# A four-layer graph network on one core: another order between graphs, adjacency in four pieces, elu without GpSimd

## The chip, the core and the metric

One core of a Trainium2 chip runs the whole program. The time is device microseconds of one execution, as a median of several; the profile page belongs to one further execution. TensorE (PE) does the matrix products, VectorE (DVE) and ScalarE (ACT) the element-wise work, GpSimd (POOL) small things, and SyncE (SP) issues transfers.

## What is computed

32 independent graphs of 512 nodes with 256 features each pass four layers. Each layer normalizes the features, takes relu, runs a graph attention, and adds its result to the features. All arithmetic is in float32.

```python
def reference(x, adj, ...):                 # x: 32 x 512 x 256, adj: 32 x 512 x 512 int32
    # layer 0: score = (h W_att) h^T / 16, softmax under the mask, two tanh convolutions
    h = relu(layernorm(x));  x = x + L0(h, adj)
    # layer 1: e = leaky(src_i + dst_j), masked softmax, attention @ Wh
    h = relu(layernorm(x));  x = x + L1(h, adj)
    # layer 2: e = exp(-leaky(s_i + d_j)) where adj != 0, rows divided by their sum, then elu
    h = relu(layernorm(x));  x = x + elu((e @ Hh) / rowsum)
    # layer 3: logits = Ax_j + Ay_i + h a_12 h^T, leaky, masked softmax, two products, then elu
    h = relu(layernorm(x));  x = x + elu(h W_1 + (attention @ h) W_2)
```

elu(y) is y for y > 0 and exp(y) - 1 otherwise. It can be written max(y, 0) + min(exp(y), 1) - 1.

## The kernel before

The kernel describes every graph as a list of small operations, each with an engine, a cost that the author took as typical, and the operations it comes after. A plan then fixes, ahead of the run, in which order each engine gets them. Up to four graphs are in flight, and the features of a fifth may be loaded. On the chip each engine runs its list strictly in order and waits where an input isn't there. The plan decides only the order; the chip decides the times.

```python
class Plan:
    PASS = 200.0
    SLACK = {"V": (1.05, 0.0), "A": (1.05, 0.0), "G": (1.5, 0.0), "D": (1.0, 800.0)}
    ...
    def order(self, pools):
        ...
        for o in reversed(self.ops):
            o["way"] += o["cost"][1] + self.PASS          # way: cost to the end of its graph
            o["rank"] = (o["graph"], -o["way"], o["number"])
            for a in o["after"]:
                if a["graph"] == o["graph"]:
                    a["way"] = max(a["way"], o["way"])
        ...                                               # each engine takes its ready operation of lowest rank
```

Loads are issued from GpSimd (only those of graph 0 from SyncE). SyncE issues the transposing transfers: of the class codes of the adjacency (codeT), of the normalized features in two 16-bit planes (planesT), and of a row of maxima (crest).

```python
def fetch(what):
    T[what] = loaded.pop((what, b)) if b == 0 else load(what, b, nc.gpsimd)

got_x = op("G", G_LOAD_X, [ends[b - FLIGHT - 1]] if b > FLIGHT else [], partial(fetch, "x"))
got_adj = op("G", G_LOAD_ADJ, [code_before], partial(fetch, "adj"))        # 1 MB in one transfer
```

Layer norm, before each layer's products: statistics and variance on DVE, the power -0.5 on GpSimd, offset on DVE, relu and scale on ACT, split in planes on DVE, transposing transfer, and the join into hT on ACT.

```python
def root(g):
    nc.gpsimd.tensor_tensor(T[f"rstd{l}"][:, two(g)], T[f"ve{l}"][:, two(g)], mhalf[:, two(g)], ALU.pow)   # L379
def norm(t):
    nc.scalar.activation(T[f"xn{l}"][:, t, :], T["x"][:, t, :], AF.Relu, bias=..., scale=...)              # L386
def split(t, place):
    nc.vector.tensor_copy(p, bits)                                                                         # L392
def turn(t, place):
    nc.sync.dma_start_transpose(out=p, in_=...)                                                            # L397
def join(t):
    nc.scalar.copy(bits[...], ...)                                                                         # L401
```

The products by name: fp features (layers 0 and 3), vp values with score columns, qk and gk the score matrices, row the scores transposed onto all partitions, av attention times values, zp and op the second convolution of layer 0, hw the own features of layer 3. In layers 1 and 2 the scores become eT through two ACT operations (L478, L482) and one masking operation on DVE (L614, L649).

The elu of layer 2 and of layer 3:

```python
# layer 2, per tile t of 128 nodes
def lower():   nc.vector.tensor_scalar(y2[t], av2[t], rs2[t], 0.0, ALU.mult, ALU.min)               # L661
def upper():   nc.scalar.activation(r2[t], av2[t], AF.Relu, scale=rs2[t])                           # L665
# per pair g of tiles
def exp2(g):   nc.scalar.activation(y2[g], y2[g], AF.Exp)                                           # L671
def add_r(g):  nc.gpsimd.tensor_add(x[g], x[g], r2[g])                                              # L674
def add_e(t):  nc.vector.scalar_tensor_tensor(x[t], y2[t], -1.0, x[t], ALU.add, ALU.add)            # L678
# layer 3, per pair
def lower3(g): nc.vector.tensor_scalar(r3[g], y3[g], 0.0, None, ALU.min)                            # L783
def upper3(g): nc.vector.scalar_tensor_tensor(x[g], y3[g], 0.0, x[g], ALU.max, ALU.add)             # L786
def exp4(g):   nc.scalar.activation(r3[g], r3[g], AF.Exp)                                           # L790
def both(g):   nc.vector.scalar_tensor_tensor(y3[g], r3[g], -1.0, x[g], ALU.add, ALU.add)           # L793
```

Of the kernel before, what the change touches and what calls it, by code (L numbers as in the profile page):

```python
# [11 lines left out]
F32 = mybir.dt.float32  # L12
I32 = mybir.dt.int32
# [6 lines left out]
P = 128  # L20
# [14 lines left out]
    return t, t + 170.0  # L35


V_STATS, V_XN, V_TINY, V_TWO, V_SCALE5 = (525.0, 610.0), (322.0, 407.0), (80.0, 165.0), (255.0, 340.0), (402.0, 486.0)
V_MASK, V_CODE, V_HALF, V_PSUM, V_ADD = (602.0, 683.0), (600.0, 690.0), (600.0, 690.0), (395.0, 484.0), (334.0, 425.0)
A_COPY, A_HALF, A_PRELU, A_EXP, A_TANH = (477.0, 597.0), (253.0, 373.0), (570.0, 693.0), (519.0, 640.0), (373.0, 474.0)  # L40
A_BIAS, A_PRELU2 = (570.0, 687.0), (629.0, 722.0)
G_POW, G_ADD, G_STORE = (981.0, 1017.0), (1230.0, 1267.0), (900.0, 900.0)
A_NORM, A_JOIN, V_SPLIT = (491.0, 590.0), (620.0, 767.0), (332.0, 422.0)
D_TURN = (1310.0, 2600.0)
G_LOAD_X, G_LOAD_ADJ = (1000.0, 6000.0), (1000.0, 9000.0)


class Plan:
# [2 lines left out]

    PASS = 200.0

    SLACK = {"V": (1.05, 0.0), "A": (1.05, 0.0), "G": (1.5, 0.0), "D": (1.0, 800.0)}

    def __init__(self):
# [22 lines left out]
    def order(self, pools):  # L81
        free = {pool: list(range(n)) for pool, n in pools.items()}
        users = {}
        for o in self.ops:
            o["left"] = len(o["after"])
            for a in o["after"]:
                users.setdefault(a["number"], []).append(o)
        for o in reversed(self.ops):
            o["way"] += o["cost"][1] + self.PASS
            o["rank"] = (o["graph"], -o["way"], o["number"])  # L90
            for a in o["after"]:
                if a["graph"] == o["graph"]:
                    a["way"] = max(a["way"], o["way"])
        engines = sorted({o["engine"] for o in self.ops})
        ready = {e: [] for e in engines}
        at = dict.fromkeys(engines, 0.0)
        events = []
        numbers = itertools.count()
        for o in self.ops:
            if not o["left"]:  # L100
                heapq.heappush(ready[o["engine"]], (o["rank"], o))
        now, out = 0.0, []
        while True:
            for e in engines:
                skipped = []
                while at[e] <= now and ready[e]:
                    rank, o = heapq.heappop(ready[e])
                    need = [p["pool"] for p in o["takes"]]
                    if any(len(free[n]) < need.count(n) for n in need):
                        skipped.append((rank, o))  # L110
                        continue
                    for p in o["takes"]:
                        p["number"] = free[p["pool"]].pop(0)
                    holds, until = o["cost"]
                    at[e] = now + holds
                    out.append(o)
                    heapq.heappush(events, (at[e], next(numbers), None))
                    heapq.heappush(events, (now + until + self.PASS, next(numbers), o))
                for x in skipped:
                    heapq.heappush(ready[e], x)  # L120
            if not events:
                break
            now = events[0][0]
            while events and events[0][0] <= now:
                o = heapq.heappop(events)[2]
                if o is None:
                    continue
                for r in o["reads"]:
                    r["readers"] -= 1
                    if not r["readers"]:  # L130
                        free[r["pool"]].append(r["number"])
                for w in users.get(o["number"], []):
                    w["left"] -= 1
                    if not w["left"]:
                        heapq.heappush(ready[w["engine"]], (w["rank"], w))
        assert len(out) == len(self.ops), "the plan is stuck"
        return out, now
# [3 lines left out]
def kernel(  # L141
# [41 lines left out]
    ps = ctx.enter_context(tc.tile_pool(name="ps", bufs=1, space=PSUM))  # L183


    def load(what, b, queue):
        if what == "x":
            t = io.tile([P, NT, H], F32, tag="x", name=f"x_{b}")
            queue.dma_start(out=t, in_=x[b].rearrange("(t p) h -> p t h", p=P))
        else:  # L190
            t = io.tile([P, NT, N], I32, tag="adj", name=f"adj_{b}", bufs=1)
            queue.dma_start(out=t, in_=adj[b].rearrange("(t p) m -> p t m", p=P))
        return t

    loaded = {("x", 0): load("x", 0, nc.sync), ("adj", 0): load("adj", 0, nc.sync)}


    ident = const.tile([P, P], F32, tag="ident", name="ident")
# [67 lines left out]

    zero = const.tile([P, 1], F32, tag="zero", name="zero")
    nc.gpsimd.memset(zero, 0.0)
    transposed(l1_sb, l1_aug[:, :, :H])
    for o in range(2):  # L270
        product(lambda d: l1_aug[:, d, H + o : H + o + 1], l1_sb,
# [43 lines left out]
    def graph(b, before, code_before):  # L315
# [25 lines left out]
            return slice(2 * g, 2 * g + 2)  # L341


        def fetch(what):
            T[what] = loaded.pop((what, b)) if b == 0 else load(what, b, nc.gpsimd)

        got_x = op("G", G_LOAD_X, [ends[b - FLIGHT - 1]] if b > FLIGHT else [], partial(fetch, "x"))
        got_adj = op("G", G_LOAD_ADJ, [code_before], partial(fetch, "adj"))

        def classes(g):  # L350
            nc.vector.tensor_scalar(T["code"][:, two(g), :], T["adj"][:, two(g), :], -1.0, 2.0, ALU.max, ALU.min)
# [3 lines left out]

        turned, code, rows_code = [], None, plan.place("code")
        for g in range(NT // 2):
            code = op("V", V_CODE, begin + [got_adj, code], partial(classes, g), takes=[] if code else [rows_code])
            turned += [op("D", D_TURN, [code], partial(turn_code, t), reads=[rows_code]) for t in (2 * g, 2 * g + 1)]

        def mask0():
# [291 lines left out]
        def third(t, a, place):  # L653
            def sums():
                rs = T["rs2"][:, t : t + 1]

                nc.vector.tensor_scalar(rs, T[f"av2{t}"][:, H : H + 1], LEAST, None, ALU.max)
                nc.vector.reciprocal(rs, rs)

            def lower():  # L660
                nc.vector.tensor_scalar(T["y2"][:, t, :], T[f"av2{t}"][:, :H], T["rs2"][:, t : t + 1], 0.0,  # L661
                                        ALU.mult, ALU.min)

            def upper():
                nc.scalar.activation(T["r2"][:, t, :], T[f"av2{t}"][:, :H], AF.Relu, scale=T["rs2"][:, t : t + 1])  # L665

            a = op("V", V_TWO, [a], sums)
            return (op("V", V_PSUM, [a], lower, reads=[place]), op("A", A_TANH, [a], upper, reads=[place]))

        def exp2(g):  # L670
            nc.scalar.activation(T["y2"][:, two(g), :], T["y2"][:, two(g), :], AF.Exp)  # L671

        def add_r(g):
            nc.gpsimd.tensor_add(T["x"][:, two(g), :], T["x"][:, two(g), :], T["r2"][:, two(g), :])  # L674

        def add_e(t):
            xt = T["x"][:, t, :]
            nc.vector.scalar_tensor_tensor(xt, T["y2"][:, t, :], -1.0, xt, ALU.add, ALU.add)  # L678

        free, us = attend(2, es, vs, third)  # L680
        xs = []
        for g in range(NT // 2):
            a = op("A", A_EXP, [l for l, _ in us[two(g)]], partial(exp2, g))
            r = op("G", G_ADD, [u for _, u in us[two(g)]], partial(add_r, g))
            xs += [op("V", V_ADD, [a, r], partial(add_e, 2 * g + j)) for j in range(2)]

# [64 lines left out]
        for g in range(NT // 2):  # L753
# [8 lines left out]
                                         l3_w1s[:, c, :], start=(c == 0), stop=(c == HC - 1))  # L762

            def own_out(g):
                nc.scalar.copy(T["w3"][:, two(g), :].rearrange("p t h -> p (t h)"), T[f"hw{g}"])

            a = op("PE", pe(n256=8), [*hs[two(g)], hi[0]], partial(own, g, place), takes=[place])
            hv.append(op("A", A_COPY, [a], partial(own_out, g), reads=[place]))


        def fourth(t, a, place):
# [7 lines left out]
            a = op("V", V_TINY, [a], sums)  # L779
            return op("V", V_PSUM, [a, hv[t // 2]], both_terms, reads=[place])  # L780

        def lower3(g):
            nc.vector.tensor_scalar(T["r3"][:, two(g), :], T["y3"][:, two(g), :], 0.0, None, ALU.min)  # L783

        def upper3(g):
            nc.vector.scalar_tensor_tensor(T["x"][:, two(g), :], T["y3"][:, two(g), :], 0.0, T["x"][:, two(g), :],  # L786
                                           ALU.max, ALU.add)

        def exp4(g):
            nc.scalar.activation(T["r3"][:, two(g), :], T["r3"][:, two(g), :], AF.Exp)  # L790

        def both(g):
            nc.vector.scalar_tensor_tensor(T["y3"][:, two(g), :], T["r3"][:, two(g), :], -1.0,  # L793
                                           T["x"][:, two(g), :], ALU.add, ALU.add)

        _, us = attend(3, es, vs, fourth)
        last = []
        for g in range(NT // 2):
            l = op("V", V_SCALE5, us[two(g)], partial(lower3, g))
            u = op("V", V_MASK, us[two(g)], partial(upper3, g))  # L800
            l = op("A", A_EXP, [l], partial(exp4, g))
            last.append(op("V", V_MASK, [l, u], partial(both, g)))

        def store():
# [45 lines left out]
```

The softmax here doesn't subtract the row's maximum and nothing guards it: scores larger than these inputs give would overflow.

## Time and profile before

| | |
|---|---|
| time, median of 3 | 2651.21 us (2650.39 to 2652.82) |
| span of the profiled execution | 2653.5 us |
| TensorE clock granted, mean | 0.983 |
| HBM read, written | 52.96 MB, 16.78 MB |
| adjacency loads from GpSimd | 31 of 1024 KB, 6.4 us median to landing |
| feature loads from GpSimd | 31 of 512 KB, 5.0 us |
| turns of planes from SyncE | 512, 2.5 us |

A group on the page reads: line, engine, operation, output <- input, shape, count, then busy time and mean ns of one, then the idle time of the engine just before it and what ended most of it. In the page's row of slices each digit is the busy share of one fortieth of the span in tenths. A line of waits reads: who waited, for whom, microseconds in total, how many times, the longest. In the table of windows each engine has its busy time and its number of instructions, and after the engines come the granted TensorE clock, the busy share of the transfer engines and GB/s.

### The profile page before, as it was taken

The numbers are of one execution on the slowest core, as the hardware profiler recorded it, in microseconds if no ns is written. First come the engines' busy times: TensorE is split into PE (matmuls) and PEld (weight loads), VectorE is DVE, ScalarE is ACT, GpSimd is POOL, SyncE is SP. The second block draws the span as 40 slices with busy tenths as digits, with TensorE's granted clock in tenths as the row PEclk, the third lists the DMA queues.
The fourth block names the chain that finished last, engine by engine and source line by source line (L and its number), as shares of the span: only waits on it lengthen the run. The fifth ranks groups of instructions, "written<-read, shape, count | busy, mean of one in ns | idle before, by whom it ended". The sixth has DMA issues, their size and how long they took to land. (4 is left out here: it accounts for less than half of the span.)

```text
span 2653.5 us, 30679 instructions
## 1 busy us (share of the span) xinstructions
PE 2531.3 (95%) x9548; PEld 1793.5 (68%) x9548; DVE 1713.0 (65%) x5174; ACT 1612.9 (61%) x3041; POOL 367.5 (14%) x426
## 2 busy tenths in 40 slices
PE   5999999999999999999999999999999999999986
PEld 4677767767667666766666776766776667666664
DVE  4467766666676666766567765666766667656664
ACT  2466766676666566665566656666666656656563
POOL 1011111011111011111111110111111111101110
PEclk8999999999999999999999999999999999999998
DMA  5323322123332223332233313233222332222111
GB/s 160 71 37 71 76 70 66 39 58 76 70 70 52 46 67 70 74 64 45 51 72 72 72 37 60 68 72 71 59 51 52 74 66 69 50 58 41 36 36 28
DMA packets 406035, 164.07 MB, mean 62 GB/s; under 512 B 386288, under 2 KB 389360, under 8 KB 405872
## 3 DMA queue, kind: packets, MB, share of 16 engines
q1 hardware_dynamic: 384032, 93.94, 19.4%
q0 software_dynamic: 17504, 65.54, 8.1%
q10 hardware_dynamic: 4336, 2.63, 0.4%
q8 instruction: 76, 1.25, 0.2%
q14 instruction: 87, 0.71, 0.1%
HBM read 52.96 MB, written 16.78 MB: 26 GB/s over the span
## 5 line engine op out<-in xcount | busy, mean ns | idle before, releaser
L501 PE MATMUL av<-v,eT 128*128 128x257 f32 x4096 | 1000.4, 385 | 39.3 <-DVE eT L614 24.2
L501 PEld LDWEIGHTS av<-v,eT 128*128 128x128 f32 x4096 | 779.3, 192 | 239.7 <-issue 97.3
L401 ACT COPY hT<-planesT 128x512 uint16<-128x512 uint16 x512 | 377.5, 765 | 131.1 <-DMA planesT<-planes 130.5
L379 POOL TENSOR_TENSOR rstd<-ve,mhalf 128x2 f32<-128x2 f32 x256 | 213.7, 851 | 1662.3 <-DVE ve L376 1417.7
L453 PE MATMUL vp<-l_aug,hT 128*128 128x258 f32 (+1 forms) x1536 | 397.7, 389 | 39.5 <-ACT hT L401 39.5
L453 PEld LDWEIGHTS vp<-l_aug,hT 128*128 128x128 f32 x1536 | 294.0, 194 | 123.4 <-ACT hT L401 53.5
L386 ACT ACTIVATE xn<-x,off,rstd 128x256 f32<-128x256 f32 x512 | 281.8, 595 | 92.8 <-DVE off L382 92.4
L392 DVE COPY planes<-xn 128x512 uint16<-128x512 uint16 x512 | 213.5, 428 | 101.4 <-ACT xn L386 79.2
L460 ACT COPY v<-vp 128x256 f32<-128x256 f32 x384 | 141.4, 373 | 177.1 <-PE vp L453 138.2
L568 PE MATMUL zp<-eT,y 128*128 128x512 f32 x512 | 241.3, 594 | 3.4 <-ACT y L557 3.3
L457 DVE COPY sd<-vp 128x2 f32<-128x2 f32 (+1 forms) x384 | 56.8, 155 | 289.9 <-ACT v L460 163.3
L538 PE MATMUL qk<-fa,hT 128*128 128x512 f32 x512 | 239.1, 592 | 0.0
L700 PE MATMUL gk<-hT,fa 128*128 128x512 f32 x512 | 224.9, 592 | 0.0
L372 DVE BATCH_NORM_STATS2 st<-x 128x6 f32<-128x256 f32 x512 | 209.1, 408 | 8.2 <-DMA x<-in_x_dram 8.2
L478 ACT ACTIVATE eT<-row,sd 128x512 f32<-128x512 f32 x256 | 164.4, 688 | 42.5 <-PE row L474 42.5
L700 PEld LDWEIGHTS gk<-hT,fa 128*128 128x128 f32 x512 | 97.2, 190 | 111.9 <-issue 106.9
L704 DVE SCALAR_TENSOR_TENSOR eT<-gk,sd,mask 128x512 f32<-128x512 f32 x128 | 96.0, 750 | 116.1 <-PE gk L700 116.0
L482 ACT ACTIVATE eT<-eT 128x512 f32<-128x512 f32 x256 | 151.8, 636 | 0.0
L542 ACT ACTIVATE eT<-qk 128x512 f32<-128x512 f32 x128 | 75.2, 598 | 123.9 <-PE qk L538 123.9
L568 PEld LDWEIGHTS zp<-eT,y 128*128 128x128 f32 x512 | 94.8, 191 | 80.1 <-issue 67.0
L736 ACT ACTIVATE eT<-eT,zero 128x512 f32<-128x512 f32 x128 | 85.3, 715 | 99.1 <-DVE crest L714 99.1
L538 PEld LDWEIGHTS qk<-fa,hT 128*128 128x128 f32 x512 | 93.7, 190 | 75.7 <-issue 67.5
(88 smaller groups left out, 3114.6 us busy)
## 6 DMA issues: line engine op xcount, KB each, us to landing
adj<-in_adj_dram POOLq DMA_DIRECT2D x31, 1024.0 KB, 6.4
out_dram<-y POOLq DMA_DIRECT2D x32, 512.0 KB, 3.4
x<-in_x_dram POOLq DMA_DIRECT2D x31, 512.0 KB, 5.0
planesT<-planes SPq DMA_TRANSPOSE x512, 2.5
codeT<-code SPq DMA_TRANSPOSE x128, 3.2
adj<-in_adj_dram SPq DMA_DIRECT2D x1, 1024.0 KB, 11.7
crest<-crest SPq DMA_TRANSPOSE x64, 2.4
x<-in_x_dram SPq DMA_DIRECT2D x1, 512.0 KB, 4.7
```

What stands on the lines that cost most here:

```text
L372: nc.vector.bn_stats(T[f"st{l}"][:, t, :], T["x"][:, t, :])
L379: nc.gpsimd.tensor_tensor(T[f"rstd{l}"][:, two(g)], T[f"ve{l}"][:, two(g)], mhalf[:, two(g)], ALU.pow)
L386: nc.scalar.activation(T[f"xn{l}"][:, t, :], T["x"][:, t, :], AF.Relu, bias=T[f"off{l}"][:, t : t + 1], scale=T[f"rstd{l}"][:, t : t + 1])
L392: nc.vector.tensor_copy(p, bits)
L401: nc.scalar.copy(bits[:, :, :, t * P : (t + 1) * P], T[f"planesT{l}{t}"].rearrange("p (b c) n -> p b c n", b=2))
L453: nc.tensor.matmul(p[:, :cols], T[f"hT{l}"][:, c, t * P : (t + 1) * P], w_aug[:, c, :], start=(c == 0), stop=(c == HC - 1))
L478: nc.scalar.activation(T[f"eT{l}"][:, c, :], T[f"row{l}"], AF.Prelu, bias=T[f"sd{l}"][:, 1, c : c + 1], alpha=ALPHA)
L482: nc.scalar.activation(e, e, AF.Exp, scale=sign)
L501: nc.tensor.matmul(p[:, : H + 1], T[f"eT{l}"][:, c, t * P : (t + 1) * P], v[:, c, :], start=(c == 0), stop=(c == NT - 1))
L538: nc.tensor.matmul(p, T["hT0"][:, k, c * P : (c + 1) * P], T["fa0"][:, k, :], start=(k == 0), stop=(k == HC - 1))
L568: nc.tensor.matmul(p, T["y0"][:, c, k * P : (k + 1) * P], T["eT0"][:, c, :], start=(c == 0), stop=(c == NT - 1))
L700: nc.tensor.matmul(p, T["fa3"][:, k, c * P : (c + 1) * P], T["hT3"][:, k, :], start=(k == 0), stop=(k == HC - 1))
```

## The change

Four things are changed.

1. **Order.** The rank of an operation is no longer (graph, way left) but one number: graph times 40 us, minus the way left. Operations of neighbouring graphs are equal in rank when the younger one has 40 us more to go. For the last graphs the distance is 10 us. The aim is that the graphs in flight keep a fixed distance, so that they are in different layers at any time.
2. **Loads.** All loads are issued by SyncE, and a graph's adjacency comes in four pieces of 256 KB; the class codes of a pair of tiles need only their two pieces. Loads of graph 0 are operations of the plan like the others.
3. **Elu of layer 2.** ACT takes exp and relu straight from the product, DVE adds min(exp, 1) and relu - 1 to the features. GpSimd adds nothing any more, and nothing is done by pairs.
4. **Elu of layer 3.** The -1 is put into w3 by a bias when ACT copies it out, so y3 holds y - 1; exp gets a bias of 1, and the separate minimum is gone.

The assumed cost of the power on GpSimd is lowered too (981/1017 to 800/850 ns), which touches the order alone.

```diff
+    APART, APART_LAST = 40000.0, 10000.0
...
+        last = max(o["graph"] for o in self.ops)
         for o in reversed(self.ops):
             o["way"] += o["cost"][1] + self.PASS
-            o["rank"] = (o["graph"], -o["way"], o["number"])
+            late = max(0, o["graph"] - last + 2)
+            o["rank"] = ((o["graph"] - late) * self.APART + late * self.APART_LAST - o["way"], o["number"])
...
-        got_x = op("G", G_LOAD_X, [ends[b - FLIGHT - 1]] if b > FLIGHT else [], partial(fetch, "x"))
-        got_adj = op("G", G_LOAD_ADJ, [code_before], partial(fetch, "adj"))
+        got_x = op("D", D_X, [ends[b - FLIGHT - 1]] if b > FLIGHT else [], fetch_x)
+        got_adj = [code_before]
+        for t in range(NT):
+            got_adj.append(op("D", D_ADJ if b else D_ADJ0, got_adj[-1:], partial(fetch_adj, t)))
...
-            code = op("V", V_CODE, begin + [got_adj, code], partial(classes, g), takes=[] if code else [rows_code])
+            code = op("V", V_CODE, begin + [got_adj[2 * g + 2], code], partial(classes, g), takes=[] if code else [rows_code])
...
             def lower():
-                nc.vector.tensor_scalar(T["y2"][:, t, :], T[f"av2{t}"][:, :H], T["rs2"][:, t : t + 1], 0.0,
-                                        ALU.mult, ALU.min)
+                nc.scalar.activation(T["y2"][:, t, :], T[f"av2{t}"][:, :H], AF.Exp, scale=T["rs2"][:, t : t + 1])
...
+            def add_lower():
+                xt = T["x"][:, t, :]
+                nc.vector.scalar_tensor_tensor(xt, T["y2"][:, t, :], 1.0, xt, ALU.min, ALU.add)
+
+            def add_upper():
+                xt = T["x"][:, t, :]
+                nc.vector.scalar_tensor_tensor(xt, T["r2"][:, t, :], -1.0, xt, ALU.add, ALU.add)
...
-        def exp2(g):
-            nc.scalar.activation(T["y2"][:, two(g), :], T["y2"][:, two(g), :], AF.Exp)
-
-        def add_r(g):
-            nc.gpsimd.tensor_add(T["x"][:, two(g), :], T["x"][:, two(g), :], T["r2"][:, two(g), :])
...
             def own_out(g):
-                nc.scalar.copy(T["w3"][:, two(g), :].rearrange("p t h -> p (t h)"), T[f"hw{g}"])
+                nc.scalar.activation(T["w3"][:, two(g), :].rearrange("p t h -> p (t h)"), T[f"hw{g}"], AF.Identity,
+                                     bias=minus)
...
-        def lower3(g):
-            nc.vector.tensor_scalar(T["r3"][:, two(g), :], T["y3"][:, two(g), :], 0.0, None, ALU.min)
...
         def exp4(g):
-            nc.scalar.activation(T["r3"][:, two(g), :], T["r3"][:, two(g), :], AF.Exp)
+            nc.scalar.activation(T["r3"][:, two(g), :], T["y3"][:, two(g), :], AF.Exp, bias=one)
```

## The prediction

> **What bounds the kernel now.** I read the page's engine totals and its row of 40 slices first, then a table of windows, then the waits of TensorE alone, then the timeline. The totals and the TensorE row:
>
> ```profile
> PE 2531.3 (95%) x9548; PEld 1793.5 (68%) x9548; DVE 1713.0 (65%) x5174; ACT 1612.9 (61%) x3041; POOL 367.5 (14%) x426
> ...
> PE   5999999999999999999999999999999999999986
> ```
>
> TensorE is busy 95%, nothing else above 68%. But "busy" at which pace? The timeline, in a stretch without gaps, gives the pitch (start, duration, line, group; the next start minus this one, over the count):
>
> ```profile
> 68.28 1.03 PE L501 MATMUL av<-v,eT 128*128 128x257 f32 x4
> 69.14 1.89 PE L523 MATMUL vp<-w_sb,hT 128*128 128x256 f32 x8
> 70.87 1.03 PE L501 MATMUL av<-v,eT 128*128 128x257 f32 x4
> ```
>
> 0.86/4 = 0.217 us for 257 columns (unrounded), 1.73/8 = 0.216 for 256. The same reading elsewhere gives 0.430 for 512 columns and 0.110 for the 128-column transposes. With the counts of the groups: 5632 of 257 or 258 columns x 0.217 = 1222; 1536 of 256 x 0.216 = 332; 2048 of 512 x 0.430 = 881; 256 transposes x 0.110 = 28; the 76 of the prologue 10. Sum **2472.6 us**, which the change doesn't touch: it neither adds nor removes a matmul. So 2653.5 - 2472.6 = **180.9 us** is what can be won at all, and the question is where it lies.
>
> The trace has all 9548 matmuls, and TensorE runs them in program order, so I laid them on a scale of pitch time and read off how far that scale moved in each stretch. Lost (stretch minus progress): 0 to 100 us 39.4; 100 to 500 -0.3, so there TensorE runs at exactly its pitch; 500 to 2500 93.4; 2500 to the end 48.4. The windows (PE, PEld, DVE, ACT, POOL busy; clock; DMA) show the same shape:
>
> ```profile
> 200.00:300.00 100.00, 100.00 (x408) 75.30 (x407) 72.71 (x212) 68.98 (x132) 13.71 (x15) 1.00 0.26 55
> ...
> 1000.00:1100.00 100.00, 95.60 (x361) 68.50 (x360) 68.07 (x206) 61.02 (x117) 15.19 (x18) 0.97 0.32 66
> ...
> 2000.00:2100.00 100.00, 94.62 (x352) 66.21 (x352) 61.85 (x189) 63.38 (x122) 12.59 (x14) 0.98 0.30 60
> ...
> 2500.00:2600.00 100.00, 87.58 (x336) 62.73 (x334) 64.76 (x193) 59.87 (x113) 11.99 (x13) 0.97 0.15 30
> 2600.00:2654.00 54.00, 31.66 (x88) 20.42 (x88) 19.46 (x46) 16.16 (x28) 2.29 (x3) 0.75 0.13 34
> ```
>
> Neither DVE nor ACT is fuller where TensorE stalls than at 200 us where it doesn't. These are latency gaps, not another engine's bound. TensorE's waits name them:
>
> ```profile
> PE vp L453 <- ACT hT L401: 39.5, 22, 6.2
> PE av L501 <- DVE eT L614: 24.2, 15, 3.9
> PE wpp L263 <- DMA l_ac<-in_L_gnn_a_dram: 18.2, 1, 18.2
> PE av L501 <- ACT eT L742: 7.3, 2, 6.9
> ```
>
> By form, 38.4 of the 39.5 are the 257-column kind: layer 3's first product, waiting for the layer norm behind layer 2. L614 is the mask of layer 1. And the tail:
>
> ```profile
> 2604.41 2.08 PE L453 MATMUL vp<-l_aug,hT 128*128 128x257 f32 x4 [6.15 <-ACT hT L401]
> 2607.61 2.08 PE L453 MATMUL vp<-l_aug,hT 128*128 128x257 f32 x4 [1.13 <-ACT hT L401]
> ...
> 2616.71 1.03 PE L453 MATMUL vp<-l_aug,hT 128*128 128x257 f32 x4
> ...
> 2634.99 10.25 PE L501 MATMUL av<-v,eT 128*128 128x257 f32 x32 [6.92 <-ACT eT L742]
> ```
>
> The last graph runs alone; after a gap the same four matmuls take 2.08 us instead of 1.03.
>
> **What the skill says.** "TensorE: Matmul & The Clock Gate", HAM oscillation: a gap longer than about 3.4 us drops the clock to half until TensorE has been busy again. The trace agrees (2.08 against 1.03), so a gap costs more than its length: in 500 to 2500 the waits add up to about 61 us, the loss is 93. "Perfetto Trace Analysis", Optimization Strategy: where the contended engine changes between regimes, interleave them. Layers 0 and 3 here are TensorE's, layers 1 and 2 ACT's (below). "GPSIMD Engine Reference", Engine selection: elementwise adds belong on VectorE. The trace agrees: 1272 ns for the add at L674, 684 ns for a 128x512 add on DVE at L786. "DMA: Bandwidth & Descriptors", Issuing engines are not separate DMA queues: moving a load to another issuer gives no bandwidth. No run before tests that.
>
> **Part 1, the order.** Rank was (graph, -way): the oldest graph always first. Now it is graph x 40 us - way, so a younger graph overtakes an older one that has less left to do. I compared both programs' TensorE order on the pitch scale. Before, every graph looks different. After, graphs 4 to 26 repeat one pattern of 76.9 us, with four graphs at four different layers. Distance on TensorE from the last producer to the first consumer, before (graphs 10 to 25) and after (steady):
> - av of layer 2 to vp of layer 3: 7 to 14 us, **36.7 after**
> - transposed scores to av, layer 1: 2.6 to 5.2, then 5.2
> - av of layer 1 to vp of layer 2: -6 to 12 (pairs overlap), then 17.3
> - op to vp of layer 1: 16 to 20, then 15.0
> - gk to av of layer 3: 15 to 17, then 21.9
> - fp to qk: 2.6 to 21, then 1.9; zp to op: 1.8 to 19, then 2.7
>
> The chain behind the first is, from the groups' means: sums 0.31, relu 0.47, GpSimd add 1.27, DVE add 0.42, statistics 0.59, variance 0.18, root 0.85, offset 0.19, norm 0.60, planes 0.43, turn 2.5, join 0.77: 8.6 us, plus queueing. It doesn't fit 7 us and fits 36.7 four times. Layer 1's chain (0.69 + 0.64 + 0.72 = 2.05 us, plus queueing) was tight at 2.6 and isn't at 5.2. The two that shrink are one copy each (0.59 us); before, zp to op at 1.8 cost 0.6 us in all, fp to qk nothing. So both large waits vanish, and with them the clock drops. I leave 8 us of the 93.4: **-85**.
>
> **Part 2, the end.** The last graphs get a distance of 10 us, so 29, 30 and 31 go abreast: their last av end at 2454, 2465 and 2473 on the pitch scale, against 2396, 2448 and 2473. Behind TensorE's end stay about 8 us (now 2645.2 to 2653.5). But layers 1 and 2 now bunch: between its copies of vp13 and vp20 of graph 31, ACT has 58 instructions, about 0.47 us each back to back = 27 us, beside 26 us of TensorE work; never fully packed, I give 10 us. Two edges are short (0.1 and 0.9 us for a chain of 2.05): 4. Low clock after these: 4. 8 + 10 + 4 + 4 = 26 instead of 48.4: **-22**.
>
> **Part 3, the loads.** Four x loads of 0.5 MB leave GpSimd's queue for SyncE's, and adjacency comes in pieces. The first 20 us move 292 GB/s over three queues, and TensorE waits 18.2 us for a vector on ACT's queue. With two queues ACT's share should rise; I guess 4 us. Then at 39.2 us GpSimd issued 1 MB of adjacency into graph 0's turns (6.8 us to land, median 2.5) and fp waited 3.5 us; now those turns go before graph 1's first piece: 3.5 us. Against this about 4 us for new tight places between 100 and 130 (row to av of layer 2 in graph 0 at 1.7 us). 39.4 becomes 36: **-3.5**. In the steady state SyncE gets 160 loads of about 0.5 us issue, 80 us in all, on a queue that isn't bound.
>
> **Part 4, the elu.** Off GpSimd go 64 adds (81.4 us) and 62 load issues (49.3). DVE: L661's 56.2 and L783's 26.8 go, 128 adds of 0.415 = 53.1 come: -30. ACT: L671's 40.4 goes, 128 exps of 0.473 = 60.5 come; biases lengthen w (0.58 to about 0.68) and r: +30. The chain becomes 7.7 us. With 36.7 us of room that is worth nothing in the middle, and ACT at 1643 us stays under 65%: **0**, or a us at the tail, inside part 2.
>
> **Sum.** 2472.6 + 36 + 8 + 26 = **2543 us**.
>
> **Rivals.** (a) The gaps move: some edge of the fixed pattern is short on the chip, say a turn stuck behind an adjacency piece on SyncE's queue. The pattern repeats some 25 times, so 2 us a graph cost 50: about 2593. For it: SyncE now mixes loads and turns in one queue. Against: 100 to 500 us shows no loss with distances no larger. (b) ACT becomes the bound in the middle, +30 us of work and an in-order engine: about 2580. Against: 51 us of ACT in a period of 77. (c) The start gets worse: SyncE waits for landings between loads and holds graph 0's turns: +10, 2553. (d) Everything hides and the end packs too: 2520.
>
> **Range and chances.** The 2472.6 and about 8 us at the end are sure, the start's 30 nearly. What is open mostly adds. I take 2520 to 2585; two per cent faster is 2598, which needs rival (a) to miss.
>
> **What would show it.** Right: windows from 200 to 2300 with PE at 99 to 100 and clock 1.00; the waits on L453 and L614 below 10 us in sum; the last vp of layer 3 without a 6 us gap; about 77 us from one store to the next. Part 3 right: the first matmul before 18 us. Wrong: a wait that shows up 25 to 28 times, or ACT over 70% there.

## The result, and the profile after

| | before | after |
|---|---|---|
| median | 2651.50 us | **2539.45 us** |
| range | 2650.39 to 2652.82 (4 runs) | 2536.70 to 2540.03 (4 runs) |
| ratio | | **0.9575**, 95% interval 0.9559 to 0.9592 |
| profiled execution | 2653.5 us | 2534.9 us, granted clock 0.994 |

112 us came off; 108 were predicted. The page of the changed kernel, engine totals and the row of slices:

```profile
PE 2489.7 (98%) x9548; PEld 1784.5 (70%) x9548; DVE 1676.7 (66%) x5110; ACT 1630.0 (64%) x3105; POOL 259.1 (10%) x302
...
PE   7999999999999999999999999999999999999998
```

TensorE went from 95 to 98% busy, and only the first slice is below 8 tenths. VectorE lost 36 us of work and ScalarE gained 17; over the shorter span their shares went from 65 to 66% and from 61 to 64%.

The windows (PE, PEld, DVE, ACT, POOL busy; clock; DMA share; GB/s) answer those shown of before:

```profile
1000.00:1100.00 100.00, 100.00 (x376) 70.08 (x375) 64.86 (x196) 63.61 (x120) 9.59 (x11) 1.00 0.27 66
...
2000.00:2100.00 100.00, 100.00 (x376) 69.97 (x375) 64.67 (x196) 63.76 (x121) 9.58 (x11) 1.00 0.31 66
...
2400.00:2500.00 100.00, 94.19 (x357) 67.87 (x356) 69.16 (x216) 76.51 (x150) 7.71 (x10) 0.97 0.17 37
2500.00:2535.00 35.00, 26.71 (x118) 22.02 (x116) 19.81 (x43) 11.60 (x18) 2.31 (x3) 0.94 0.17 53
```

At 1000 and at 2000 us TensorE has no gap and the full clock, with the other engines about as full as before. From 2400 to 2500 ScalarE rises to 76.5: the last graphs' layers 1 and 2 bunch towards the end. In the three stretches of 10 us around TensorE's longest waits there, ScalarE is full or nearly, and at 2320 VectorE too:

```profile
2320.00:2330.00 10.00, 5.30 (x15) 4.08 (x16) 9.60 (x33) 10.00 (x20) 3.43 (x4) 0.66 0.51 119
2400.00:2410.00 10.00, 6.47 (x26) 5.11 (x25) 6.67 (x17) 9.28 (x18) 0.80 (x1) 0.83 0.13 28
2440.00:2450.00 10.00, 7.80 (x30) 6.13 (x29) 6.40 (x25) 9.97 (x21) 1.06 (x1) 0.83 0.32 53
```

TensorE's waits (in total, times, longest):

```profile
PE wpp L267 <- DMA l_ac<-in_L_gnn_a_dram: 13.3, 1, 13.3
PE av L517 <- DVE eT L630: 8.5, 3, 4.2
PE vp L539 <- ACT hT L417: 5.3, 1, 5.3
```

The two large waits of before, on the line of vp (39.5 us, 38.4 of them layer 3's) and on layer 1's mask (24.2 us), became 2.1 (none of it layer 3's) and 8.5 us; the 8.5 lie at the start (1.1) and at the end (7.4).

I use the pitch scale of the prediction again: the time of a stretch minus the pitch time of the matmuls done in it is what TensorE lost there. In us, for the two kernels and the experiments up to e5, which are described below:

| kernel | 0-100 | 100-250 | 250-2350 | 2350-end | sum | median time |
|---|---|---|---|---|---|---|
| before | 39.4 | -0.1 | 90.5 | 51.1 | 181 | 2651.5 |
| after | 27.3 | 9.2 | 7.0 | 19.0 | 62.5 | 2539.5 |
| order alone (e1) | 37.8 | -0.1 | 10.7 | 21.0 | 69 | 2545.1 |
| loads and elu, old order (e2) | 29.9 | 17.7 | 11.0 | 46.8 | 105 | 2579.6 |
| order and elu, old loads (e3) | 37.0 | -0.1 | 8.3 | 18.6 | 64 | 2539.1 |
| order and loads, old elu (e4) | 29.1 | 10.4 | 6.9 | 18.2 | 65 | 2538.8 |
| before without adjacency loads (f1) | 33.1 | 0.3 | 37.7 | 50.6 | 122 | 2597.9 |
| loads alone (f2) | 29.7 | 18.8 | 25.2 | 58.4 | 132 | 2606.1 |
| elu alone (f3) | 38.5 | 0.6 | 45.1 | 55.6 | 140 | 2615.4 |
| 40 us at the end (e5) | 30.8 | 9.5 | -1.5 | 44.3 | 83 | 2557.6 |

Where the new order has its 7 to 11 us in the column 250-2350, they lie after 2300 us and belong to the end (after: -1.2 from 250 to 2300, 27.2 from there on); only e1 loses some 4 us before 2300.

### The profile page after: what moved, and what is told of

Read it like the earlier page. It is cut to its first block, busy times and chain, and to the rows that moved or that the text cites. A ratio compares the mean times of both kernels' runs of the same rounds, so it can differ in the third digit from the quotient of the medians.

```text
span 2534.9 us, 30658 instructions
## 1 busy us (share of the span) xinstructions
PE 2489.7 (98%) x9548; PEld 1784.5 (70%) x9548; DVE 1676.7 (66%) x5110; ACT 1630.0 (64%) x3105; POOL 259.1 (10%) x302
## 4 chain that ended last, share of the span: by engine, by line
PE 94%; issue 3%; DVE 2%; ACT 1%; DMA 0%; POOL 0%; POOLq 0%; ACTq 0%
PE av L517 33%; PE vp L469 13%; PE zp L584 9%; PE qk L554 9%; PE fp L444 8%; PE gk L712 8%; PE vp L539 4%; PE op L603 4%; PE hw L773 4%; PE row L490 1%; PE wpp L267 1%; DVE st L388 0%; DMA l_ac<-in_L_gnn_a_dram 0%; DMA w_sb<-in_L_gnn_W_dram 0%; ACT eT L494 0%
## 5 line engine op out<-in xcount | busy, mean ns | idle before, releaser
L517 PE MATMUL av<-v,eT 128*128 128x257 f32 x4096 | 960.6, 381 | 15.3 <-DVE eT L630 8.5
L395 POOL TENSOR_TENSOR rstd<-ve,mhalf 128x2 f32<-128x2 f32 x256 | 232.7, 910 | 2055.7 <-DVE ve L392 1984.7
L417 ACT COPY hT<-planesT 128x512 uint16<-128x512 uint16 x512 | 384.5, 773 | 72.3 <-DMA planesT<-planes 70.7
L469 PE MATMUL vp<-l_aug,hT 128*128 128x258 f32 (+1 forms) x1536 | 378.1, 381 | 2.1 <-ACT hT L417 2.1
L402 ACT ACTIVATE xn<-x,off,rstd 128x256 f32<-128x256 f32 x512 | 290.9, 608 | 44.3 <-DVE off L398 43.8
L554 PE MATMUL qk<-fa,hT 128*128 128x512 f32 x512 | 233.9, 592 | 0.0
L539 PE MATMUL vp<-w_sb,hT 128*128 128x256 f32 x512 | 122.9, 383 | 5.3 <-ACT hT L417 5.3
L539 PEld LDWEIGHTS vp<-w_sb,hT 128*128 128x128 f32 x512 | 96.1, 192 | 39.3 <-issue 23.1
```

The lines of the kernel that those rows point to most:

```text
L417: nc.scalar.copy(bits[:, :, :, t * P : (t + 1) * P], T[f"planesT{l}{t}"].rearrange("p (b c) n -> p b c n", b=2))
L469: nc.tensor.matmul(p[:, :cols], T[f"hT{l}"][:, c, t * P : (t + 1) * P], w_aug[:, c, :], start=(c == 0), stop=(c == HC - 1))
L517: nc.tensor.matmul(p[:, : H + 1], T[f"eT{l}"][:, c, t * P : (t + 1) * P], v[:, c, :], start=(c == 0), stop=(c == NT - 1))
L539: nc.tensor.matmul(p[:, j * H : (j + 1) * H], T["hT0"][:, c, t * P : (t + 1) * P], w0_sb[:, c, :], start=(c == 0), stop=(c == HC - 1))
L554: nc.tensor.matmul(p, T["hT0"][:, k, c * P : (c + 1) * P], T["fa0"][:, k, :], start=(k == 0), stop=(k == HC - 1))
```

## The experiments

Each ran four times beside the kernel before on the same chip. Before's median was 2652.3 with e1 to e4, 2653.6 with f1 to e5, 2653.0 with e6, e7 and g2, 2649.6 with e9.

### Each part put in or taken out (e1 to e4)

Theory: the order makes the time; loads and elu are worth a few us. Rival: the loads or the elu do part of it by shortening the chain itself.

**e1, the order alone**: before, with the new rank.

```diff
-            o["rank"] = (o["graph"], -o["way"], o["number"])
+            late = max(0, o["graph"] - last + 2)
+            o["rank"] = ((o["graph"] - late) * self.APART + late * self.APART_LAST - o["way"], o["number"])
```

> The kernel before with the new rank alone (loads and elu as before). Theory D, the distance on TensorE between producer and consumer is what counts: the loss of 93 us in the middle goes wholly, the start stays at 39 us and has some tight places behind it (about 10 us: in this order the distance from op to vp of layer 1 is 1.0 us in graph 3), the end loses about 27: 2472 + 39 + 10 + 0 + 27 = 2548 us (2538 to 2560). Rival U, the shorter elu and the loads carry the gain: about 2620 us or more.

Measured: 2545.05 us (2543.57 to 2546.46), ratio 0.9596 (0.9582 to 0.961). The order alone brings 107 of the 112 us.

**e2, everything but the order**: after, with the old rank (the same diff backwards).

> The changed kernel with the old rank (oldest graph first): loads from SyncE in pieces and the new elu alone. Theory D: the start gains some 10 us, the chain is 0.9 us shorter, but the distances from av of layer 2 to vp of layer 3 are again 5 to 12 us and uneven, so the middle loses about 90 us and the end about 48: 2472 + 30 + 90 + 48 = 2640 us (2620 to 2660). Rival U: near 2560 us.

Measured: **2579.59 us** (2577.63 to 2582.42), ratio 0.9727 (0.9711 to 0.9744). This expectation missed by 60 us. With the old order, loads and elu together (and the lowered assumed cost of the power, which e2 keeps) bring 73 us, and TensorE's middle loses 11 us instead of 90. So my reason was incomplete: the middle can be freed by the order, and also without it.

**e3, the old loads in the changed kernel** (1 MB of adjacency and x on GpSimd's queue):

```diff
-            got_adj.append(op("D", D_ADJ if b else D_ADJ0, got_adj[-1:], partial(fetch_adj, t)))
+        got_adj = op("G", G_LOAD_ADJ, [code_before], partial(fetch, "adj"))
```

> The changed kernel with the loads of before (GpSimd, adjacency in one piece of 1 MB). Theory: only the start knows the loads. TensorE's first matmul goes back from 13.3 to about 18 us and graph 0's first products to about 41 to 48 us; start loss 39 instead of 27, the middle loses nothing, the end 27: 2545 us (2538 to 2555). Rival: the 1 MB pieces disturb the turns in the middle too, some us per graph: 2580 us or more.

Measured: 2539.11 us (2538.07 to 2541.16), ratio 0.9575 (0.956 to 0.9589), the same as after. The table says why: the start to 100 us is 10 us worse, 37.0 instead of 27.3, and the filling from 100 to 250 is 9 us better, nothing instead of 9.2.

**e4, the old elu in the changed kernel** (the removed lines of the diff put back):

```diff
-                nc.vector.scalar_tensor_tensor(xt, T["r2"][:, t, :], -1.0, xt, ALU.add, ALU.add)
+            nc.gpsimd.tensor_add(T["x"][:, two(g), :], T["x"][:, two(g), :], T["r2"][:, two(g), :])
```

> The changed kernel with both elus of before (GpSimd additions, minimum before exp). Theory: with 16 us and more of TensorE work between av of layer 2 and vp of layer 3 the longer chain is hidden; the same time as the changed kernel within 8 us: 2540 us (2534 to 2550). Rival: GpSimd's additions of 1.27 us hold up its roots, or the shorter chain was needed: 2560 us or more.

Measured: 2538.76 us (2538.06 to 2540.28), ratio 0.9573 (0.9559 to 0.9587): the elu is worth nothing on top of the rest. e3 and e4 are both 6 us faster than e1. Each of them has one of the two small parts, and both have the lowered assumed cost of the power, which e1 has not; so which of the three brings the 6 us is not shown. By the table they lie after 250 us: e1 loses 31.7 us from there on, e3 26.9 and e4 25.1.

### What filled the chain under the old order (f1 to f3)

e2 asked for a new theory. In before's trace I looked at one of the long waits. GpSimd issues a 1 MB load of adjacency:

```profile
1021.45 0.97 POOL L192 DMA_DIRECT2D adj<-in_adj_dram  x1
```

Just then SyncE issues the turns of layer 3's norm:

```profile
1022.84 1.26 SPq L397 DMA_TRANSPOSE planesT<-planes  x1
1024.14 1.87 SPq L354 DMA_TRANSPOSE codeT<-code  x1
1026.11 4.49 SPq L397 DMA_TRANSPOSE planesT<-planes  x3
```

ScalarE waits for them, and TensorE for ScalarE:

```profile
1030.02 0.76 ACT L401 COPY hT<-planesT 128x512 uint16<-128x512 uint16 x1 [3.93 <-DMA planesT<-planes]
```
```profile
1030.83 2.08 PE L453 MATMUL vp<-l_aug,hT 128*128 128x257 f32 x4 [3.54 <-ACT hT L401]
```

The turn of 1022.84 lands 7.2 us later, just before its use at 1030.02; the median is 2.5. Theory C: the 1 MB loads collide with the turns. Rival E: the chain is long by itself, through the GpSimd addition and the queues.

**f1, before without the adjacency loads.** The order on every engine stays before's. All graphs use graph 0's adjacency, so 31 loads of 1 MB are left out, and with them GpSimd's time to issue them (0.97 us in the line above); the output is another.

```diff
-            T[what] = loaded.pop((what, b)) if b == 0 else load(what, b, nc.gpsimd)
+            if what == "adj":
+                T[what] = loaded[("adj", 0)]
+            else:
+                T[what] = loaded.pop((what, b)) if b == 0 else load(what, b, nc.gpsimd)
```

> The kernel before with its order, its elu and its GpSimd queue as they were; only the 31 adjacency loads of 1 MB for graphs 1 to 31 are left out (every graph uses graph 0's adjacency, so the output is not the reference's). Theory C (the middle was lost because the 1 MB load collides with the turns of layer 3's norm, which then land late, once or twice a graph): most of the 93 us in the middle goes, 2570 to 2600, with layer 3's vp waiting below 15 us in sum. Rival E (the chain behind layer 2 is long by itself, through the GpSimd addition and the queues on the engines, and loads have little to do with it): 2630 to 2650, vp still waiting 30 us or more.

Measured: 2597.9 us (2595.84 to 2601.72), ratio 0.9797 (0.9779 to 0.9816). The same product of the same graph, in f1 (start, duration, and no wait):

```profile
1013.46 1.03 PE L456 MATMUL vp<-l_aug,hT 128*128 128x257 f32 x4
```

The wait and the half clock after it are gone. What ScalarE waits for turns in the whole run (us, times) is, in before,

```profile
  DMA planesT<-planes: 130.5, 101
```

and in f1

```profile
  DMA planesT<-planes: 71.6, 93
```

Of the middle's 90.5 us, 37.7 stay.

**f2, the loads alone** (before with x and four pieces of adjacency on SyncE, old elu, old rank; the loads' part of the diff).

> The kernel before with the loads alone changed: x and adjacency by SyncE, adjacency in pieces of 256 KB; old elu, old order by graph number. Theory C: the pieces are short and lie apart, so the turns no longer stick behind one; about 2580 to 2605, near the 2579.6 that loads and elu together gave. Rival E: 2625 to 2645, only the start's few us are gained.

Measured: 2606.1 us (2604.88 to 2607.71), ratio 0.9827 (0.9807 to 0.9847), just outside the range of theory C and far from the rival's. The middle falls to 25.2. The start's filling and the end get worse by 19 and 7 us, which is why f1 is faster though its middle is not.

**f3, the elu alone** (before with both elus changed, GpSimd still issuing the 1 MB loads, old rank).

> The kernel before with both elus alone changed (no GpSimd addition, the -1 in a bias); GpSimd still issues the loads of 1 MB, old order by graph number. Theory C: 2625 to 2650, since the collision stays. Rival E: 2585 to 2605, since the chain gets shorter by the GpSimd addition and GpSimd is free for the root.

Measured: 2615.42 us (2614.35 to 2616.22), ratio 0.9861 (0.9845 to 0.9878): between the two expectations, so neither theory alone is right. The wait on the line of layer 3's vp (total, times, longest; 39.5 us in before) is in f3

```profile
PE vp L460 <- ACT hT L408: 25.0, 27, 6.9
```

and in f1

```profile
PE vp L456 <- ACT hT L404: 11.3, 8, 6.2
```

I then measured the chain itself, for graphs 8 to 27: from the last av of a pair of layer 2's tiles to the end of the join that layer 3's first vp on this pair needs, whether TensorE waits for it or not. The room beside it is TensorE's other work between these two products, on the pitch scale. In us, the chain as a median:

| kernel | chain, first pair | room, first pair | chain, second pair | room, second pair |
|---|---|---|---|---|
| before | 21.3 | 16.0 to 23.0 | 19.7 | 15.0 to 19.5 |
| before without adjacency loads (f1) | 17.7 | 16.0 to 23.0 | 17.4 | 15.0 to 19.5 |
| elu alone (f3) | 16.5 | 14.2 to 19.1 | 15.3 | 13.4 to 15.8 |
| loads and elu, old order (e2) | 15.2 | 14.2 to 19.2 | 13.5 | 12.1 to 20.7 |
| after | 22.8 | 43.6 to 47.1 | 18.6 | 39.3 to 42.7 |

So **both are true**. Without the loads the chain is 2 to 4 us shorter (over 5 in some graphs), with the shorter elu 4 to 5; with the loads in pieces and the elu it mostly fits the old order's room (which shrinks a little where the plan knows of a shorter elu), and the first pair's vp waits visibly (0.5 us) in one graph of twenty. The changed kernel's chain is about as long as before's; it has about twice its length in room.

That it is the transfer which suffers, and not a root that GpSimd starts late because it issues a load, the same instructions show: in before the turn of the first pair is issued 13.9 us after the av and lands 5.4 us later, in f1 it is issued after 13.8 and lands 2.4 us later (medians). From 250 to 2300 us before's turns that are issued within 6 us after an adjacency load take 5.0 us to land, the others 2.4; with pieces of 256 KB from SyncE (f2) both take 2.3.

In e1 ScalarE waits for turns even longer than before,

```profile
  DMA planesT<-planes: 151.7, 129
```

and the turns behind a load of 1 MB take 4.4 us against 2.4: the collision is still there. TensorE loses some 4 us from 250 to 2300, 3.2 of them where a turn took 8.5 us (2244 us); elsewhere the collision is hidden.

### The end (e5)

```diff
-    APART, APART_LAST = 40000.0, 10000.0
+    APART, APART_LAST = 40000.0, 40000.0
```

> The changed kernel with 40 us instead of 10 us between the last graphs, one number. If the end's gain comes from the last graphs running abreast, the end loses about 45 to 50 us again instead of 27 and the time is 2555 to 2570, all of it after 2300 us. Rival (the end is set by the regular pattern alone, the shorter distance adds nothing): 2535 to 2545.

Measured: 2557.55 us (2557.31 to 2557.66), ratio 0.9643 (0.9627 to 0.966). All of it lies at the end: from 250 us on it loses 42.8 us instead of 26.0. The last graph runs alone again, and both waits of before's tail are back:

```profile
2508.49 3.79 PE L469 MATMUL vp<-l_aug,hT 128*128 128x257 f32 x8 [9.04 <-ACT hT L417]
...
2538.32 8.95 PE L517 MATMUL av<-v,eT 128*128 128x257 f32 x32 [6.91 <-ACT eT L754]
```

The second number of the change is worth 18 us by itself.

### Is the room real? A root eight times as long (e6, e7, e9)

If 37 to 44 us of room make the chain harmless, a chain made longer on purpose must be harmless too.

```diff
-                nc.gpsimd.tensor_tensor(T[f"rstd{l}"][:, two(g)], T[f"ve{l}"][:, two(g)], mhalf[:, two(g)], ALU.pow)
+                for _ in range(8 if l == 3 else 1):
+                    nc.gpsimd.tensor_tensor(T[f"rstd{l}"][:, two(g)], T[f"ve{l}"][:, two(g)], mhalf[:, two(g)], ALU.pow)
```

**e6, in the changed kernel, its order untouched.**

> The changed kernel with the root of layer 3's norm computed 8 times on GpSimd instead of once (7 more of about 0.85 us for each pair of tiles, so the chain behind layer 2 is 6 us longer for the first pair and up to 12 for the second; same order on every engine). If the order's room between layer 2's last product and layer 3's first (37 us on the pitch scale) is what makes the chain harmless, the middle still loses nothing and the time is 2540 to 2565. Rival (the room is used up by queueing, the chain is just barely hidden): 2650 or more.

Measured: **2799.73 us** (2798.99 to 2803.21), ratio 1.0554 (1.0532 to 1.0576). Missed by 235 us.

**e7, in the kernel before, its order untouched.**

> The kernel before with the same 8 roots in layer 3's norm and its own order. The same 6 to 12 us now fall on edges with 16 to 23 us of room that were already waiting: 6 to 11 us more for each of 32 graphs, 2850 to 3000. Rival (the old order also hides it somewhere else, since another graph's products stand between): below 2750.

Measured: 2875.15 us (2873.7 to 2878.27), ratio 1.0837 (1.0814 to 1.086). The old order pays 222 us for the longer root, the new one 260. The new order forgives a wrong duration no better than the old. In e7 the line of layer 3's vp waits 63.6 us for its norm, the largest of TensorE's waits.

TensorE's largest wait in e6 says where:

```profile
PE av L518 <- DVE eT L631: 141.0, 31, 5.8
```

It isn't layer 3's product that waits, but the av of another graph's layer 1, for VectorE's mask. And VectorE waits for

```profile
DVE off L399 <- POOL rstd L396: 326.1, 122, 6.2
```

In VectorE's timeline of e6 (L392 is the variance, L399 the offset):

```profile
1002.16 0.16 DVE L392 TENSOR_SCALAR ve<-mv 128x2 f32<-128x2 f32 x1
...
1004.20 0.18 DVE L389 BATCH_NORM_AGGREGATE mv<-st 128x2 f32<-128x6 f32 x1
1008.62 0.16 DVE L399 SCALAR_TENSOR_TENSOR off<-mv,rstd 128x2 f32<-128x2 f32 x1 [4.24 <-POOL rstd L396]
...
1011.03 1.29 DVE L631 TENSOR_TENSOR eT<-eT,mask 128x512 f32<-128x512 f32 x2
```

The plan had put the offset a few instructions behind the variance in VectorE's queue, where a root of 0.8 us would be done. VectorE stands there for 4.24 us, and the mask L631 of the other graph, which needs nothing from this root, stands behind it. So e6's reasoning failed at the queue: the room between two matmuls is no room for an instruction that stands early in an in-order queue.

**e9, the same, with an order planned for the real length.**

```diff
-                r = op("G", G_POW, [a], partial(root, g))
+                r = op("G", (8 * G_POW[0], 8 * G_POW[1]) if l == 3 else G_POW, [a], partial(root, g))
```

> The changed kernel with the same 8 roots in layer 3's norm, and this time the order is planned with the root's real length (one number). With the root eight times as long but the old plan it took 2799.7 us: VectorE reached the offset 6 instructions after the variance and stood there for the root (326 us in sum), and the masks of other graphs behind it in its queue came late. Theory (what has to have room is the place of each instruction in its own engine's queue, not the distance between matmuls alone): now about 26 instructions stand between variance and offset, VectorE no longer waits there, the middle loses nothing and the time is 2545 to 2575, with a longer start and end. Rival (GpSimd's longer chain is too much for four graphs in flight whatever the order): 2620 or more.

Measured: **2550.27 us** (2549.84 to 2550.65), ratio 0.9619 (0.9602 to 0.9636). The same instructions as e6, 249 us faster through one number of the plan. The window of e9:

```profile
1000.00:1100.00 100.00, 100.00 (x378) 70.34 (x377) 66.75 (x215) 65.75 (x123) 22.25 (x28) 1.00 0.32 79
```

and what VectorE waited for ahead of the offset in e9 (us, times):

```profile
  POOL rstd L396: 3.0, 4
```

3.0 us instead of 326.1. The remaining 11 us against after lie at the start (3.6) and the end.

### A version that beats both (g2)

After e3 the start was what was left: 36.5 us lost to 250. The timeline of after shows why graph 0 begins late (VectorE):

```profile
5.42 0.43 DVE L388 BATCH_NORM_STATS2 st<-x 128x6 f32<-128x256 f32 x1 [5.42 <-DMA x<-in_x_dram]
...
14.31 0.16 DVE L269 COPY l_aug<-wpp 128x1 f32<-128x1 f32 x1 [6.62 <-PE wpp L267]
...
26.06 0.13 DVE L398 SCALAR_TENSOR_TENSOR off<-mv,rstd 128x2 f32<-128x2 f32 x1
```

x is there at 5.4 us and GpSimd's root done at 8.6, but the offset stands at 26.06, behind the copies of the weights' products in the same queue. That looks like e6's mechanism again. In g2 these products are operations of the plan, the weights of layers 1 to 3 are loaded by GpSimd, and so are x of graphs 1 to 4. Its core:

```diff
-    transposed(l1_sb, l1_aug[:, :, :H])                    # in the prologue, ahead of graph 0
+    aug1 = transposed(l1_sb, l1_aug[:, :, :H], [got1])     # operations of the plan, after got1
...
-                a = op("PE", pe(n256=4), [hs[t]], partial(product, t, place), takes=[place])
+                a = op("PE", pe(n256=4), [hs[t]] + aug, partial(product, t, place), takes=[place])
```

> The changed kernel with the products of the weights taken out of the prologue and put into the order among graph 0's and 1's work, and with the loads that only later layers need moved to GpSimd, so that ScalarE and VectorE reach graph 0's norm first. In the changed kernel graph 0's first product starts at 35.2 us though its x has landed at 5.4; from the groups' means its norm, planes, turn and join need some 9 to 11 us more. Theory (the start is set by the in-order queues of VectorE and ScalarE standing behind the weights): first product of graph 0 at 15 to 20 us, 2515 to 2530. Rival (the start is set by what has to be moved over the DMA engines, and what is won there is lost again between 100 and 250 us): 2533 to 2545.

Measured: **2527.76 us** (2526.51 to 2529.78), ratio 0.9528 (0.9504 to 0.9551), about 12 us less than after. The order of the products and the issuer of the loads changed together, so the 12 us aren't split between them. The loss to 250 us is 27.6 instead of 36.5. TensorE's timeline of g2:

```profile
18.72 2.08 PE L566 MATMUL vp<-w_sb,hT 128*128 128x256 f32 x4 [18.72 <-ACT hT L444]
23.81 2.08 PE L566 MATMUL vp<-w_sb,hT 128*128 128x256 f32 x4 [3.01 <-ACT hT L444]
```

Graph 0 begins 16 us earlier. What holds it now is the turns, in ScalarE's timeline of g2:

```profile
17.91 0.76 ACT L444 COPY hT<-planesT 128x512 uint16<-128x512 uint16 x1 [6.22 <-DMA planesT<-planes]
23.00 0.76 ACT L444 COPY hT<-planesT 128x512 uint16<-128x512 uint16 x1 [4.33 <-DMA planesT<-planes]
```

SyncE issues the first of them at 10.53, so it takes 7.4 us, while the 16 DMA engines are busy 90% or more in most of the time from 4 to 24 us. That later loads of x and weights would let these turns through was not tried.

## Why the prediction was right, and where it wasn't

**The total.** 2543 against 2539.45. The 2472.6 us of matmuls stood; the losses were predicted as 36 + 8 + 26 = 70 and measured as 36.5 (to 250 us), -1.2 (to 2300) and 27.2, together 62.5. One of its signs of being right was missed by little: the waits on the line of layer 3's vp and on layer 1's mask sum to 10.6 us, not below 10; most of it lies at the end, and none of it is layer 3's vp.

**Part 1, the order: right in size, wrong in its sizing of the chain.** Parts 1 and 2 together were put at -107; the order alone measured -107. The middle loses nothing, where 8 us were left. But two terms were off. "From the groups' means: ... 8.6 us, plus queueing" takes 17.7 us on the chip (f1, without the adjacency loads), so what I left without a number is as much as the rest; how much of it is the pair's second tile, queues on the engines or hand-over between them was not separated. And "7 to 14 us" of room was counted from the last tile of layer 2 to the first product of layer 3, though that product waits for the first pair of tiles only; by pairs it was 15 to 23 us. The two errors cancel, so the conclusion held partly by luck. "Fits 36.7 four times" was too much: it is about twice (22.8 in 43.6).

**The cause of the middle's loss was incomplete.** The prediction called the waits latency gaps, which they are, and gave all of their removal to the order. e2, f2 and f3 show two more ways: the loads alone bring 47 us and the elu alone 38, both in before's order. The three parts alone sum to 193 us and together make 112, because they remove the same waits.

**Part 2, the end: right.** 26 predicted, 27.2 measured: 8.2 us behind TensorE's last matmul (8 predicted), some 11.5 of waits on layer 1's and layer 2's masks and the norm, the rest mostly low clock after them. "Never fully packed" was wrong for short stretches: ScalarE is full for 10 us around two of the three waits on masks, which cost 9.5 us where 10 was given for ScalarE. But VectorE is 96% busy around the longest of them, so which of the two held the masks up was not separated. e5 shows that the distance of 10 us makes it.

**Part 3, the loads: right in sum, by two errors.** To 100 us they were to bring 7.5 us (4 from the weights, 3.5 from the turns of graph 0); after against e3 it is 9.7. The first matmul starts at 13.3 instead of 18.2, and the 3.5 us wait on fp is gone. "About 4 us for new tight places" was 9.2; why the new loads cost that much between 100 and 250 us stays open. The net of -3.5 is 0.5 at the start, and nothing in the time.

**Part 4, the elu: 0, as predicted,** on top of the order (e4). VectorE lost 36 us where 30 were predicted, ScalarE gained 17 where 30 were. Alone in the old order it is worth 38 us. A part can be priced only together with what else is changed.

**The rivals.** (a) fell: no edge waits in the repeated pattern, though SyncE issues all 160 loads between the turns, and one store follows another after 76.9 us. (b) fell: ScalarE is at 64% in the middle. (c) fell in sum, but the filling of the pipeline did lose more than I gave. (d) was right of the middle and not of the end.

**The clock after a gap.** The 3.4 us of the prediction is no sharp edge here. A gap of 2.90 us in before (783.9 us) and one of 2.19 us in after (2445.3 us) were followed by nearly 4 us at half pace, one of 3.23 us in before (2547.9 us) by none.

**The issuers, against the runs.** The Trainium skill, "DMA: Bandwidth & Descriptors", Issuing engines are not separate DMA queues, says that transfers started by different engines interleave on the same 16 DMA engines. The traces agree: a load that GpSimd issued made SyncE's turn take 7.2 us, and moving all loads from one issuer to the other, with the order in place, changed nothing (2539.1 against 2539.5). Under the old order it did pay (f2), but there the 1 MB transfer was also cut in four, and no run separates the size from the issuer.

## What to carry to other kernels

In a fixed order on in-order queues, look for the room of every instruction in its own queue, and not only between matmuls: one early consumer of a late result holds up everything behind it, of other work too, and the durations that the planner assumes have to be the real ones (2800 us against 2550 through one number). A wait that ends in the middle of a long chain can be taken away by shortening the chain, by moving a transfer that collides with it, or by more distance; these remove the same microseconds, so measure each alone and on top of the others before you credit one. A gain at a pipeline's start is only a gain once it is still there when the pipeline is full.

## What the runs showed that I had not expected

- A chain of 8.6 us by the means of its instructions and transfers took about 18 us between engines that were only 61 to 68% busy.
- A 1 MB load issued 1.4 us ahead of a turn of 128 KB nearly tripled its time, 7.2 us against a median of 2.5; at the start of g2, under loads of x, adjacency and weights, one took 7.4 us.
- The new order was no more tolerant of a longer instruction than the old one (260 us against 222 lost in e6 and e7), though it has about twice the room on TensorE.
- Loads or elu, taken out of the changed kernel one at a time, change nothing; in the old order the two together are worth 73 us.
